# Layer 3's chunk sums in bf16: adjacency rows read in place with a stride, weights in three bf16 pieces

## The chip, the cores and the metric

The kernel runs on one core of one Trainium2 chip. The metric is the device time of one execution in microseconds (us). The kernel before takes 864.41 us as the median of three runs (862.12 to 865.53). TensorE is called PE below, VectorE DVE, ScalarE ACT, GpSimd POOL, and SyncE, which only issues transfers here, SP.

## The reference, cut to what matters

The program is a graph network of four layers over 2708 nodes with 128 features; the adjacency `adj` holds only zeros and ones. Each layer takes a normalised and rectified copy of `x` and adds its result to `x`. The change is in the last layer:

```
h     = max(layernorm(x), 0)
XW    = h @ W
s_col = XW @ a[:128];  s_row = XW @ a[128:]
den   = exp(leaky_relu(s_row[:, None] + s_col[None, :], 0.01))
num   = adj @ den
att   = where(num != 0, den / num, 0)
x     = x + adj @ (att @ XW)
```

`den` is not formed in full. Its entry for row i and column j is the exponential of s_row[i] + s_col[j] where that sum is positive, and of a hundredth of it elsewhere, so it factors on either side of a threshold. The kernel sorts the nodes by s_row into 22 chunks. For a column j, whole chunks lie on one side of the threshold and need only sums that do not depend on j; one chunk is cut by the threshold and is computed exactly. Those sums are the chunk sums: for each of the 22 chunk edges, the sum over the adjacency's rows of `exp(0.01 r)` times the rows below the edge, and of `exp(r)` times the rows above it. That is one product of a 44-column weight matrix with the transposed adjacency.

## The kernel before, in words

The nodes are held as T = 22 tiles of 128 (the last has 20). Layers 0, 1 and 2 come first; a flag then chooses between two copies of the rest, and the profiled execution takes the one with `exact` true, in which every adjacency entry is exactly representable in bf16.

Layer 3 runs in these steps. Ranks are counted (lines 728 to 776). From the ranks come the masks `ge` and `lt` (lines 791 and 793, 22 by 22 or 23 per partition) and the weights `wts` (lines 794 and 795): mask times `r_low` or `r_exp`, in f32. Then `sums(t)` (lines 798 to 816) loads one row tile of the transposed adjacency, 128 by 2708 in f32, over SP's queue, and multiplies it with `wts[:, t, :]`: six f32 matmuls of 44 weight columns and some 452 moving columns. They go to three banks of PSUM, `accs`; each bank has a lower half at partition 0 and an upper half at partition 64, and the two matmuls of a bank use different columns of the array.

The rows have four kinds of place. The first four tiles use `early_rows`, buffers that are free early. Tiles 8, 19 and 20 (`LATER`) use the buffers `hs`, `hT` and `row_b`, the last two of which are needed before for the tables. The rest take turns in the four buffers of `steps`.

Beside the sums runs a long chain, mostly of small DVE instructions: the first table (`placed("k", ...)`, line 870: products on DVE, then 22 matmuls at line 854), its reading (`joined`), the chunk edges (matmul, line 875), a count of the columns per chunk (lines 880 to 899), a plan that packs the columns into steps (lines 924 to 1005), the second table (`placed("j", ...)`, line 1008), and the indices of rows and prefix sums. Then `densities` (lines 1070 to 1091) makes 44 small matrices in 11 calls, four at a time: a product on DVE (line 1074), an f32 matmul (line 1081) into one of two PSUM banks, and its evacuation by DVE and ACT in turn (lines 1087 and 1089), a maximum and an exponential. Lines 1093 to 1100 call densities, the remaining sums and the gathers of adjacency rows. When the last sum is done, `accs` is copied out, cut in a high and a low part (lines 1107 to 1111) and sent to DRAM (`pre_d`, line 1114). The loop over 22 steps that follows (from line 1125) needs rows gathered out of `pre_d` before it can begin; it ends with the products of lines 1191 and 1135. A last product with the adjacency (line 225) finishes the layer.

The order of the instructions on each engine is set by a planner: it walks the program with its own costs, and gives an engine the earliest instruction in program order among those that it holds to be ready. Later ones can so slip in where an engine would be idle. A few stages are kept in program order by hand; the stage of the change is not.

`pieces` (line 832) cuts an f32 vector into bf16 parts: a cast, a subtraction of the cast from the rest, and so on. It is used before for the two tables.

Of the kernel before, what the change touches and what calls it, by code (L numbers as in the profile page):

```python
# [8 lines left out]
F32 = mybir.dt.float32  # L9
BF16 = mybir.dt.bfloat16  # L10
# [4 lines left out]
ALU = mybir.AluOpType  # L15
AX = mybir.AxisListType
# [3 lines left out]
def kernel(  # L20
# [19 lines left out]
    nc = tc.nc  # L40
    P = 128
    N, D = x.shape
    assert D == P
    T = -(-N // P)
# [6 lines left out]
    BLK = list(zip(CUTS[:-1], CUTS[1:]))  # L51
# [10 lines left out]
    def rows(t):  # L62
        return min(P, N - t * P)
# [23 lines left out]
    const = ctx.enter_context(tc.tile_pool(name="const", bufs=1))  # L87
    big = ctx.enter_context(tc.tile_pool(name="big", bufs=1))
    small = ctx.enter_context(tc.tile_pool(name="small", bufs=2))
    stage = ctx.enter_context(tc.tile_pool(name="stage", bufs=4))  # L90
    ps_acc = ctx.enter_context(tc.tile_pool(name="ps_acc", bufs=1, space=bass.MemoryType.PSUM))
    ps = ctx.enter_context(tc.tile_pool(name="ps", bufs=2, space=bass.MemoryType.PSUM))

# [3 lines left out]
    def acc_bank(b):  # L97
        return ps_acc.tile([P, 512], F32, tag=f"acc{b}", name=f"acc{b}")
# [59 lines left out]
    hn = big.tile([P, T, D], F32, name="hn")  # L158
    hT = big.tile([P, NPAD], F32, name="hT")
    hs = big.tile([P, T, P + 2], F32, name="hs")  # L160
    yT = big.tile([P, NPAD], F32, name="yT")
# [5 lines left out]
    dflat = big.tile([P, max(2 * N, NS * P)], F32, name="dflat")  # L167
# [107 lines left out]
    with ExitStack() as stack:  # L275
# [23 lines left out]
        for b in range(NB):  # L299
            layernorm(b, hn)  # L300
            p = bank()
            turned(p, hn, TILES[b])
            nc.vector.tensor_copy(hT[:, spans(b)], p[:, : len(TILES[b]) * P])
            p = acc_bank(b % 2)
            w = len(TILES[b]) * P
# [28 lines left out]
        accs = [acc_bank(b) for b in range(NB)]  # L334
# [13 lines left out]
        for t in range(T):  # L348
            a = first_rows[t] if t < 3 else load_rows(adj, t)
            late = t >= T - 2  # L350
            rhs = (yT, row_b)[t % 2]
            for h, (h0, h1) in enumerate(COLS):
                w = h1 - h0
# [11 lines left out]
                for b in range(3 * h, 3 * h + 3):  # L365
                    lo, hi = E0[b]
# [5 lines left out]
                        start=(t == 0 and b < GR),  # L372
                        stop=(t == T - 1 and b >= GR),
# [24 lines left out]
        p = bank()  # L398
# [36 lines left out]
    CH = P - len(SUMS)  # L435
    NC = T
# [10 lines left out]
    by_ch = iota("by_ch", [P, NC + 1], [[CH, NC + 1]], 0)  # L447
# [39 lines left out]
    def rest(exact, stack3):  # L487


        s12 = stack3.enter_context(ExitStack())  # L490
        ring = s12.enter_context(tc.tile_pool(name="ring", bufs=6))
        raws = s12.enter_context(tc.tile_pool(name="raws", bufs=4))
        h2 = hs[:, :, :P]
        if exact:
            parts = s12.enter_context(tc.tile_pool(name="parts", bufs=1))
# [73 lines left out]
        def finish1(b, acc):  # L569
            evacuate(b, yT, acc)  # L570
            n = len(TILES[b])
            p = bank()
            o = stage.tile([P, 4, P], F32, tag="o", name="o", bufs=2)
            for q, t in enumerate(TILES[b]):
                nc.tensor.matmul(p[:, cols(q)], yT[:, cols(t)], w1_sb, start=True, stop=True)
            for q, t in enumerate(TILES[b]):
                nc.scalar.activation(o[:, q, :], p[:, cols(q)], AF.Relu, scale=dis[:, t : t + 1])
            ts = slice(TILES[b][0], TILES[b][-1] + 1)
            nc.vector.tensor_add(xs[:, ts, :], xs[:, ts, :], o[:, :n, :])
            layernorm(b, h2)  # L580
            if b >= 3:
                cut_in_two(h2, b)
# [52 lines left out]
        steps = stack3.enter_context(tc.tile_pool(name="steps", bufs=4))  # L635
# [8 lines left out]
        r_exp = keepers.tile([P, T], F32, name="r_exp")  # L644
# [10 lines left out]
        regained = [b[:, :N] for b in (hT, row_b, hs.rearrange("p t w -> p (t w)"), yT)]  # L655
# [13 lines left out]
        with tc.tile_pool(name="tab", bufs=1) as tab, tc.tile_pool(name="tabs", bufs=2) as tabs:  # L669

            def tt(name, shape, a, b, op, dtype=F32, tag=None):
                o = tab.tile(shape, dtype, tag=tag or name, name=name)
                nc.vector.tensor_tensor(o, a, b, op)
                return o
# [12 lines left out]
            for b in range(NB):  # L687
                lo, hi = E0[b]
                n = len(TILES[b])
                ts = slice(TILES[b][0], TILES[b][-1] + 1)  # L690
                nc.scalar.activation(yT[:, lo:hi], row_b[:, lo:hi], AF.Relu, bias=tot[:, 6:7], scale=tot[:, 5:6])
                p = acc_bank(b % 2)
                turned(p, yT, TILES[b], True)
                f = len([t for t in TILES[b] if t < TF])
# [8 lines left out]
                p = acc_bank(2 + b % 2)  # L703
# [10 lines left out]
                for c in range(new.start, new.stop, 3):  # L714
# [8 lines left out]
                    p = acc_bank(4)  # L723
# [5 lines left out]
            for c in range(0, T, 3):  # L729
# [9 lines left out]
                for q in range(m):  # L739
                    t = c + q  # L740
                    r = rows(t)
# [14 lines left out]
                    o = (t % 4) * P  # L756
# [5 lines left out]
            p = bank()  # L762
# [4 lines left out]
            rank = tab.tile([P, T], F32, name="rank")  # L767
# [12 lines left out]
            r_low = tab.tile([P, T], F32, name="r_low")  # L780
# [1 line left out]
            nc.vector.tensor_scalar_mul(row_a[:, :N], row_b[:, :N], -0.99)  # L782


            def over(x, n):
                return x[:, :, None].to_broadcast([P, T, n])

            def along(x, n):
                return x[:, None, :].to_broadcast([P, T, n])

            ge = tt("ge", [P, T, NC + 1], over(rank, NC + 1), along(by_ch, NC + 1), ALU.is_ge)
            wts = tab.tile([P, T, 2 * NC], F32, name="wts")
            lt = tt("lt", [P, T, NC], over(rank, NC), along(by_ch[:, :NC], NC), ALU.is_lt, tag="w3")
            nc.vector.tensor_mul(wts[:, :, :NC], lt, over(r_low, NC))
            nc.vector.tensor_mul(wts[:, :, NC:], ge[:, :, 1:], over(r_exp, NC))
            accs = [acc_bank(b) for b in range(3)]

            def sums(t):
                r = rows(t)
                if t < NEARLY:  # L800
                    a = early_rows[t]
                elif t in LATER:
                    a = regained[LATER[t]]
                else:
                    a = steps.tile([P, N], F32, tag="rows", name="rows")
                nc.sync.dma_start(a[:r, :], adj_t[t * P : t * P + r, :])
                for b in range(3):
                    for h in range(2):
                        lo, hi = BLK[b + 3 * h]
                        nc.tensor.matmul(  # L810
                            accs[b][64 * h : 64 * h + 2 * NC, : hi - lo],
                            wts[:r, t, :],
                            a[:r, lo:hi],
                            start=(t == 0),
                            stop=(t == T - 1),
                        )

            early_rows = [dflat[:, :N], dflat[:, N : 2 * N], hn.rearrange("p t d -> p (t d)")[:, :N], yT[:, :N]]
            NEARLY = len(early_rows)

            LATER = {NEARLY + 4: 2, T - 3: 0, T - 2: 1}
            for t in range(NEARLY):
                sums(t)


            ohc = tt("ohc", [P, T, NC], ge[:, :, :NC], ge[:, :, 1:], ALU.subtract)
            nth = tab.tile([P, T], F32, name="nth")
            nc.vector.tensor_reduce(nth, ge[:, :, 1:NC], AX.X, ALU.add)
            slot = tab.tile([P, T], F32, name="slot")
            nc.vector.scalar_tensor_tensor(slot, nth, float(-CH), rank, ALU.mult, ALU.add)  # L830

            def pieces(name, x, n):
                out = []
                for i in range(n):
                    h = tab.tile([P, T], BF16, name=f"{name}{i}")
                    nc.vector.tensor_copy(h, x)
                    out.append(h)
                    if i < n - 1:
                        rest = tab.tile([P, T], F32, name=f"{name}r{i}")
                        nc.vector.tensor_sub(rest, x, h)  # L840
                        x = rest
                return out

            def placed(name, onehot, lanes, groups, p):

                w = len(sum(groups, [])) * NC
                hs_ = lanes[:, : T * P].rearrange("p (t q) -> p t q", q=P)
                nc.vector.tensor_tensor(hs_, along(place_of if name == "k" else lane, P), over(slot, P), ALU.is_equal)
                lo = 0 if name == "k" else 5 * NC * T
                rhs = row_b.bitcast(BF16)[:, lo : lo + T * w].rearrange("p (t s) -> p t s", s=w)  # L850
                for i, v in enumerate(sum(groups, [])):
                    nc.vector.tensor_mul(rhs[:, :, i * NC : (i + 1) * NC], onehot, over(v, NC))
                for t in range(T):
                    nc.tensor.matmul(p[:, :w], hs_[:, t, :], rhs[:, t, :], start=(t == 0), stop=(t == T - 1))

            def joined(dst, p, at, n):

                if n == 1:
                    nc.vector.tensor_copy(dst, p[:, at * NC : (at + 1) * NC])
                else:  # L860
                    nc.vector.tensor_reduce(
                        dst, p[:, at * NC : (at + n) * NC].rearrange("p (i b) -> p b i", b=NC), AX.X, ALU.add
                    )
# [5 lines left out]
            p = acc_bank(3)  # L869
            placed("k", ohc, hT.bitcast(BF16)[:, :NPAD], [r_p, node_p], p)  # L870
            ktab = tab.tile([P, 2 * NC], F32, name="ktab")
            joined(ktab[:, :NC], p, 0, 3)
            joined(ktab[:, NC:], p, 3, 2)
            p = acc_bank(4)
# [10 lines left out]
            p = acc_bank(3)  # L885
# [6 lines left out]
            for t in range(T - 1):  # L892
# [4 lines left out]
                    start=False,  # L897
# [20 lines left out]
            def sums_before(name, x):  # L918
# [66 lines left out]
                tag="w3",  # L985
# [327 lines left out]
```

## Time and profile before

| | us |
|---|---|
| median of three runs | 864.41 |
| the profiled execution | 862.16 |
| its span, first to last instruction | 860.4 |
| layer 3 from the masks to the first table's matmuls | 441.65 to 455.09 |
| from there to the first density's product | 455.09 to 494.67 |
| densities and remaining sums | 495.4 to 524.8 |
| copy-out, store, gather, first product of the loop | 524.8 to 543.6 |
| loop of 22 steps | 543.6 to 787.5 |
| last product and output | 787.5 to 860.4 |

| engine | busy us | share |
|---|---|---|
| PE | 737.2 | 86% |
| DVE | 580.9 | 68% |
| ACT | 536.0 | 62% |
| POOL | 191.8 | 22% |

The shares are over the whole span. The chunk sums (line 810) appear as 528 matmul records, two for each of 264 f32 matmuls. In the profile's answers, "idle before <- X" names what ended an engine's wait; "issue" means that it waited for nothing that the profile shows; x counts instructions. A window's row gives, for each engine, its busy us and in brackets its instructions, then the granted PE clock, the busy share of the DMA engines and the GB/s that they moved.

### The profile page before, as it was taken

What the parts mean: (1) busy time and instruction counts of PE and PEld (TensorE: products, weight loads), DVE (VectorE), ACT (ScalarE), POOL (GpSimd) and SP (SyncE); (2) the same over time, 40 slices, a digit from 0 to 9 for tenths busy, and PEclk for the clock granted to TensorE, in tenths of its full rate; (3) what the DMA queues carried; (4) which work ended last, traced back from release to release, by engine and by line L of the source; (5) the groups of instructions that cost most, each with busy time, mean ns of one, the idle gap of its engine ahead of it and who ended that gap; (6) DMA issues with size and microseconds to landing.
All of it is one profiled execution on the core that took longest, in us unless ns stands there. A gap on an engine that the chain in (4) does not pass through costs nothing.

```text
span 860.4 us, 8730 instructions
## 1 busy us (share of the span) xinstructions
PE 737.2 (86%) x2981; PEld 427.3 (50%) x2981; DVE 580.9 (68%) x1098; ACT 536.0 (62%) x595; POOL 191.8 (22%) x161
## 2 busy tenths in 40 slices
PE   3599999995996989978669893599998999989996
PEld 2333333333775867755224221456555555545785
DVE  5499879796734263458986974566666676665854
ACT  3899999995846474446940043578777777777000
POOL 3000000013201020011000101656666666620010
PEclk9899999996998989978769997799999999999999
DMA  9044544724997999967304956677777777786994
GB/s 335 3 163 161 194 172 164 291 75 172 385 397 257 361 362 396 367 260 270 115 1 178 417 203 238 235 283 261 267 271 257 274 276 270 285 313 251 421 428 132
DMA packets 39474, 218.61 MB, mean 254 GB/s; under 512 B 5107, under 2 KB 13998, under 8 KB 25358
## 3 DMA queue, kind: packets, MB, share of 16 engines
q1 hardware_dynamic: 27704, 150.19, 45.5%
q0 software_dynamic: 8624, 65.76, 21.2%
q10 hardware_dynamic: 3090, 1.99, 0.7%
q8 instruction: 26, 0.43, 0.2%
q14 instruction: 30, 0.25, 0.1%
HBM read 214.12 MB, written 3.79 MB: 253 GB/s over the span
## 4 chain that ended last, share of the span: by engine, by line
PE 17%; DMA 11%; DVE 10%; issue 6%; POOL 5%; ACT 5%; POOLq 0%; DVEq 0%; ACTq 0%
PE bank L1191 5%; DMA hs<-in_adj_t_dram 4%; PE acc L1135 4%; DMA row_b<-pre_d,pre_i 4%; PE acc L810 3%; ACT rows L1153 2%; PE acc L225 2%; PE bank L1081 2%; POOL hs L647 1%; POOL hT L647 1%; DVE bits L744 1%; POOL xw L647 1%; POOL row_b L647 1%; ACT e L1205 1%; DMA hs<-in_adj_t_dram,row_i 1%
## 5 line engine op out<-in xcount | busy, mean ns | idle before, releaser
L1191 PE MATMUL bank<-rows,d_hi 128*128 128x512 f32 (+1 forms) x264 | 105.6, 404 | 37.9 <-DVE d_hi L1160 17.4
L225 PE MATMUL acc<-rows,h_hi 128*128 128x512 f32 (+1 forms) x264 | 105.8, 405 | 11.6 <-ACT rows L529 6.3
L1135 PE MATMUL acc<-e,xw 128*128 128x512 f32 (+1 forms) x264 | 104.3, 545 | 0.0
L1196 ACT ACTIVATE ln<-bank,tiny 128x512 f32<-128x512 f32 x132 | 79.5, 632 | 31.1 <-PE bank L1191 31.1
L225 PE MATMUL acc<-rows,h_lo 128*128 128x512 f32 (+1 forms) x264 | 97.7, 386 | 0.2 <-DVE h_lo L506 0.2
L1191 PE MATMUL bank<-rows,d_lo 128*128 128x512 f32 (+1 forms) x264 | 97.4, 380 | 0.0
L1191 PEld LDWEIGHTS bank<-rows,d_hi 128*128 128x128 f32 x264 | 50.6, 192 | 67.3 <-ACT ln L1196 30.3
L1199 DVE TENSOR_TENSOR e<-e,ln 128x1536 f32<-128x1536 f32 (+2 forms) x66 | 69.7, 1096 | 14.8 <-ACT ln L1196 14.4
L359 DVE SCALAR_TENSOR_TENSOR tau<-tau,e_hi,a 128x1536 f32<-128x1536 f32 (+1 forms) x44 | 70.5, 1622 | 9.9 <-DMA a<-in_adj_dram 6.0
L1135 PEld LDWEIGHTS acc<-e,xw 128*128 128x128 f32 x264 | 48.5, 190 | 52.6 <-issue 52.6
L356 ACT ACTIVATE tau<-row_a,e_neg,e_lo 128x1536 f32<-128x1536 f32 (+1 forms) x44 | 65.7, 1504 | 3.0 <-PE bank L368 2.8
L225 PEld LDWEIGHTS acc<-rows,h_hi 128*128 128x128 f32 x264 | 52.1, 198 | 26.0 <-ACT rows L529 8.6
L368 PE MATMUL bank<-tau,ones_at 128*32 128x512 f32 (+1 forms) x264 | 51.8, 566 | 8.3 <-DVE tau L359 8.3
L225 PEld LDWEIGHTS acc<-rows,h_lo 128*128 128x128 f32 x264 | 52.0, 198 | 11.7 <-issue 1.9
L1205 ACT ACTIVATE e<-e 128x2708 f32<-128x2708 f32 x22 | 54.2, 2462 | 3.2 <-DVE e L1199 3.2
L225 PE MATMUL acc<-yT,hs 128*128 128x512 f32 x132 | 55.8, 560 | 0.0
L225 PE MATMUL acc<-row_b,hs 128*128 128x512 f32 x132 | 55.3, 557 | 0.0
L1191 PEld LDWEIGHTS bank<-rows,d_lo 128*128 128x128 f32 x264 | 51.0, 193 | 6.7
L225 PE MATMUL acc<-rows,y_hi 128*128 128x512 f32 x132 | 49.2, 379 | 4.6 <-DVE rows L1268 2.7
L225 PE MATMUL acc<-rows,y_lo 128*128 128x512 f32 x132 | 47.7, 376 | 0.0
L1174 DVE TENSOR_SCALAR xw<-xw,c_exp 128x128 f32<-128x128 f32 x22 | 6.3, 285 | 60.4 <-DMA xw<-xw_d,xw_i 60.4
L529 ACT CAST rows<-dflat 128x1536 fp32r<-128x1536 f32 (+1 forms) x26 | 34.2, 1330 | 20.2 <-DMA dflat<-in_adj_t_dram 9.7
(409 smaller groups left out, 1414.7 us busy)
## 6 DMA issues: line engine op xcount, KB each, us to landing
a<-in_adj_dram SPq DMA_DIRECT2D x21, 1354.0 KB
rows<-in_adj_t_dram SPq DMA_DIRECT2D x17, 1354.0 KB
dflat<-in_adj_t_dram SPq DMA_DIRECT2D x9, 768.0 KB
rows<-in_adj_t_dram SPq DMA_DIRECT2D x9, 768.0 KB
dflat<-in_adj_dram SPq DMA_DIRECT2D x9, 768.0 KB
rows<-in_adj_dram SPq DMA_DIRECT2D x9, 768.0 KB
dflat<-in_adj_t_dram SPq DMA_DIRECT2D x5, 1354.0 KB
hs<-in_adj_t_dram SPq DMA_DIRECT2D x5, 1354.0 KB
```

The costliest lines, as they stand in the source:

```text
L225: nc.tensor.matmul(accs[b][:, : hi - lo], w, moving[:, lo - at : hi - at], start=start and i == 0, stop=stop and i == len(parts) - 1,)
L356: nc.scalar.activation(tau[:, :w], row_a[:, h0:h1], AF.Relu, bias=e_neg[:, t : t + 1], scale=e_lo[:, t : t + 1])
L359: nc.vector.scalar_tensor_tensor(tau[:, :w], tau[:, :w], e_hi[:, t : t + 1], a[:, h0:h1], ALU.add, ALU.mult)
L368: nc.tensor.matmul(den[g : g + 32, : hi - lo], ones_at[:, b // GR, :], tau[:, lo - h0 : hi - h0], start=(t == 0 and b < GR), stop=(t == T ...
L529: m = nc.vector.tensor_copy(r, a) if i % 2 and i > 4 else nc.scalar.copy(r, a)
L647: return nc.gpsimd.indirect_dma_start(out=out, out_offset=None, in_=src, in_offset=bass.IndirectOffsetOnAxis(ap=idx, axis=0),)
L810: nc.tensor.matmul(accs[b][64 * h : 64 * h + 2 * NC, : hi - lo], wts[:r, t, :], a[:r, lo:hi], start=(t == 0), stop=(t == T - 1),)
L1135: m = nc.tensor.matmul(accs[b][:, : hi - lo], xw, e[:, lo:hi], start=(s == 0), stop=(s == NE - 1))
L1191: m = nc.tensor.matmul(num[:, : hi - lo], d, a[:, lo:hi], start=(i == 0), stop=(i == len(products) - 1))
L1196: nc.scalar.activation(ln[:, lo:hi], num[:, : hi - lo], AF.Ln, bias=tiny)
L1199: tc.keep_in_program_order(nc.vector.tensor_sub(e[:, beg:hi], e[:, beg:hi], ln[:, beg:hi]))
L1205: tc.keep_in_program_order(nc.scalar.activation(e, e, AF.Exp))
```

## The change

In the exact branch the chunk sums no longer use f32 operands. The upper 16 bits of an f32 zero or one are that number in bf16, so the loaded tile is read in place as bf16, every second element: a stride of two elements, four bytes. The weights `r_low` and `r_exp` are cut by `pieces` into three bf16 parts each, and three weight tensors `wts0` to `wts2` are built, each 44 columns wide. A bank of a row tile then takes six bf16 matmuls (three parts, two halves) where it took two in f32.

`pieces` is moved up so that it can be called there. The loop that calls `sums` for the first four tiles, with their loads, moves down: in program order it now stands behind the first table's products and matmuls, between the allocation of `ktab` and the reading of the table. The pool `stage`, which held the tile `o` of layer 1's finish, is replaced by a pool `relus` of the same two buffers, opened with the pools of layers 1 and 2.

```diff
-    stage = ctx.enter_context(tc.tile_pool(name="stage", bufs=4))
...
+        relus = s12.enter_context(tc.tile_pool(name="relus", bufs=2))
...
-            o = stage.tile([P, 4, P], F32, tag="o", name="o", bufs=2)
+            o = relus.tile([P, 4, P], F32, tag="o", name="o")
...
             ge = tt("ge", [P, T, NC + 1], over(rank, NC + 1), along(by_ch, NC + 1), ALU.is_ge)
-            wts = tab.tile([P, T, 2 * NC], F32, name="wts")
             lt = tt("lt", [P, T, NC], over(rank, NC), along(by_ch[:, :NC], NC), ALU.is_lt, tag="w3")
-            nc.vector.tensor_mul(wts[:, :, :NC], lt, over(r_low, NC))
-            nc.vector.tensor_mul(wts[:, :, NC:], ge[:, :, 1:], over(r_exp, NC))
+            values = [(r_low, r_exp)]
+            if exact:
+                values = list(zip(pieces("r_low_p", r_low, 3), pieces("r_exp_p", r_exp, 3)))
+            wts = []
+            for i, (v_low, v_exp) in enumerate(values):
+                w = tab.tile([P, T, 2 * NC], BF16 if exact else F32, name=f"wts{i}")
+                nc.vector.tensor_mul(w[:, :, :NC], lt, over(v_low, NC))
+                nc.vector.tensor_mul(w[:, :, NC:], ge[:, :, 1:], over(v_exp, NC))
+                wts.append(w)
...
                 nc.sync.dma_start(a[:r, :], adj_t[t * P : t * P + r, :])
+                if exact:
+                    a = a.bitcast(BF16).rearrange("p (n h) -> p n h", h=2)[:, :, 1]
                 for b in range(3):
-                    for h in range(2):
-                        lo, hi = BLK[b + 3 * h]
-                        nc.tensor.matmul(
-                            accs[b][64 * h : 64 * h + 2 * NC, : hi - lo],
-                            wts[:r, t, :],
-                            a[:r, lo:hi],
-                            start=(t == 0),
-                            stop=(t == T - 1),
-                        )
+                    for i, w in enumerate(wts):
+                        for h in range(2):
+                            lo, hi = BLK[b + 3 * h]
+                            nc.tensor.matmul(
+                                accs[b][64 * h : 64 * h + 2 * NC, : hi - lo],
+                                w[:r, t, :],
+                                a[:r, lo:hi],
+                                start=(t == 0 and i == 0),
+                                stop=(t == T - 1 and i == len(wts) - 1),
+                            )
...
-            for t in range(NEARLY):
-                sums(t)
...
             placed("k", ohc, hT.bitcast(BF16)[:, :NPAD], [r_p, node_p], p)
             ktab = tab.tile([P, 2 * NC], F32, name="ktab")
+            for t in range(NEARLY):
+                sums(t)
             joined(ktab[:, :NC], p, 0, 3)
```

More of the change, by code (lines that the diff above doesn't have):

```diff
@@ L782, in rest @@
             nc.vector.tensor_scalar_mul(row_a[:, :N], row_b[:, :N], -0.99)
[L785 to L791, printed above, removed]
-            wts = tab.tile([P, T, 2 * NC], F32, name="wts")
-            lt = tt("lt", [P, T, NC], over(rank, NC), along(by_ch[:, :NC], NC), ALU.is_lt, tag="w3")
-            nc.vector.tensor_mul(wts[:, :, :NC], lt, over(r_low, NC))
-            nc.vector.tensor_mul(wts[:, :, NC:], ge[:, :, 1:], over(r_exp, NC))
[L796 to L807, printed above, removed]
-                    for h in range(2):
-                        lo, hi = BLK[b + 3 * h]
-                        nc.tensor.matmul(
-                            accs[b][64 * h : 64 * h + 2 * NC, : hi - lo],
-                            wts[:r, t, :],
-                            a[:r, lo:hi],
-                            start=(t == 0),
-                            stop=(t == T - 1),
-                        )
-            early_rows = [dflat[:, :N], dflat[:, N : 2 * N], hn.rearrange("p t d -> p (t d)")[:, :N], yT[:, :N]]
-            NEARLY = len(early_rows)
-            LATER = {NEARLY + 4: 2, T - 3: 0, T - 2: 1}
-            for t in range(NEARLY):
-                sums(t)
[L826 to L830, printed above, removed]
             def pieces(name, x, n):
@@ L842, in pieces, with over, along @@
                 return out
+            def over(x, n):
+                return x[:, :, None].to_broadcast([P, T, n])
+            def along(x, n):
+                return x[:, None, :].to_broadcast([P, T, n])
+            ge = tt("ge", [P, T, NC + 1], over(rank, NC + 1), along(by_ch, NC + 1), ALU.is_ge)
+            lt = tt("lt", [P, T, NC], over(rank, NC), along(by_ch[:, :NC], NC), ALU.is_lt, tag="w3")
+            values = [(r_low, r_exp)]
+            if exact:
+                values = list(zip(pieces("r_low_p", r_low, 3), pieces("r_exp_p", r_exp, 3)))
@@ new lines, in rest, with sums @@
+            wts = []
[4 more added lines that the diff above has]
+                wts.append(w)
+            accs = [acc_bank(b) for b in range(3)]
+            def sums(t):
+                r = rows(t)
+                if t < NEARLY:
+                    a = early_rows[t]
+                elif t in LATER:
+                    a = regained[LATER[t]]
+                else:
+                    a = steps.tile([P, N], F32, tag="rows", name="rows")
+                nc.sync.dma_start(a[:r, :], adj_t[t * P : t * P + r, :])
+                if exact:
+                    a = a.bitcast(BF16).rearrange("p (n h) -> p n h", h=2)[:, :, 1]
+                for b in range(3):
+                    for i, w in enumerate(wts):
[8 more added lines that the diff above has]
+                            )
@@ new lines, in rest @@
+            early_rows = [dflat[:, :N], dflat[:, N : 2 * N], hn.rearrange("p t d -> p (t d)")[:, :N], yT[:, :N]]
+            NEARLY = len(early_rows)
+            LATER = {NEARLY + 4: 2, T - 3: 0, T - 2: 1}
+            ohc = tt("ohc", [P, T, NC], ge[:, :, :NC], ge[:, :, 1:], ALU.subtract)
+            nth = tab.tile([P, T], F32, name="nth")
+            nc.vector.tensor_reduce(nth, ge[:, :, 1:NC], AX.X, ALU.add)
+            slot = tab.tile([P, T], F32, name="slot")
+            nc.vector.scalar_tensor_tensor(slot, nth, float(-CH), rank, ALU.mult, ALU.add)
```

## The prediction

> **What bounds the kernel now.** I read the stages first. One row each for the early sums, the middle and the density stage; columns are PE, PEld, DVE, ACT, POOL busy, PE clock, DMA share, GB/s:
>
> ```profile
> 444.05:455.10 11.05, 10.99 (x49) 3.40 (x49) 7.07 (x10) 0.00 (x0) 0.00 (x0) 0.84 0.01 1
> 457.20:495.40 38.20, 33.85 (x211) 13.07 (x210) 36.37 (x101) 0.22 (x1) 4.06 (x4) 1.00 0.86 343
> 495.40:524.80 29.40, 29.33 (x94) 8.15 (x94) 21.36 (x43) 15.85 (x34) 3.00 (x3) 0.94 0.52 192
> ```
>
> Three different limits. In the first PE is full (10.99 of 11.05). In the second DVE is (36.37 of 38.20) and DMA nearly so; PE's 33.85 lies beside them. In the third PE is full again (29.33 of 29.40). Then the chain of waits (start, duration):
>
> ```profile
> 444.11 11.06 PE acc L810 x48
> 455.16 1.21 PE acc L854 x22
> 456.37 0.89 PE acc L810 x2
> ...
> 494.67 0.70 DVE diag L1074
> 495.42 3.68 PE bank L1081 x4
> 499.10 1.64 PE acc L810 x6
> 500.74 1.05 PE bank L1081 x2
> ```
>
> The sums of line 810 are on the path twice: four early tiles ahead of the first table, and the last six tiles (72 records) amid the densities. Last, PE and DVE in order of time:
>
> ```profile
> 448.55 0.12 PEld L810 LDWEIGHTS acc<-dflat,wts 128*44 128x44 f32 x2 [0.26 <-issue]
> ...
> 449.31 0.13 PEld L810 LDWEIGHTS acc<-dflat,wts 128*44 128x44 f32 x2 [0.25 <-issue]
> 449.68 0.13 PEld L810 LDWEIGHTS acc<-dflat,wts 128*44 128x44 f32 x2 [0.25 <-issue]
> ...
> 449.89 1.23 DVE L852 TENSOR_TENSOR row_b<-ohc,node_p 128x484 bf16<-128x484 f32 x2
> ...
> 522.27 2.48 PE L810 MATMUL acc<-rows,wts 20*44 20x452 f32 x12
> ```
>
> Two weight loads, one per half bank, start together every 0.377 us (448.55, 449.31, 449.68). So the halves run side by side, and a tile (12 records, six rounds) costs 6 x 0.377 = 2.26 us. The early tiles cost more since the first rounds ran at the low clock, 0.75 us each until 447.8. The first table's DVE products end at 451.12, but its matmuls start at 455.09: they stood 4.0 us behind the early sums.
>
> **The Trainium skill.** "FP8 and Floating Point Precision", TensorE Precision Notes: true f32 takes four passes, bf16 one. The trace agrees: two records of 0.377 are four passes of 0.188 us for 452 columns. "TensorE: Matmul & The Clock Gate", "Wait — 56ns, not 53.3ns?": one pass costs N / 2.4 GHz + 2.5 ns warm, so 0.191 us; the 0.188 agrees. "Advanced Engine Details and Errata", SBUF Cachelines: a stride is free while there are at least two hits on a 16-byte line. A stride of four bytes has four hits, so I expect full pace; no bf16 read with a stride is in this trace. "TensorEngine Tiling (Array Packing)", Key Properties: different tiles can load weights and multiply in parallel. The f32 pairs do.
>
> **The change part by part.**
>
> Pool `relus`: same two buffers, used only in layer 1; nothing.
>
> Pieces: six casts and four subtractions. The rows of r_p (line 836) last 0.18 us and start some 0.1 apart, so 1.0 us, from when r_exp and r_low exist (409.6, 410.5 us). There ACT's row sums (line 747) run without a break to 439.7 and DVE waits for them. Nothing; 1.0 to 1.8 us if that cover is gone.
>
> Weights: six products for two. The f32 pair starts 0.57 apart (442.82, 443.39); bf16 products of that size (line 852) last the same 0.66. Four more are +2.3 us on DVE ahead of the first table, which becomes ready at 451.1 + 2.3 = 453.4. The 4.0 us that it waited for PE hide this only if PE is free by then.
>
> Early sums: 4 tiles x 9 rounds x 0.19. The first weights exist at about 444.0, the third at 446.3. With the low clock to 447.8 about 6 of 36 rounds are done by then, and 30 x 0.19 = 5.7 us bring the end to 453.5. The text puts the table's matmuls first, but they are not ready. The planner fills an idle PE: at 456.3 it set sums of a late tile ahead of line 875's matmul, which precedes them in the program. So I expect most early sums before the table. Its matmuls then start at 453.5 against 455.09: -1.6 us. Whatever sums the planner leaves between the table and the chunk-edge matmul (line 875) hold that one up, and behind it the whole DVE chain to 494.67. All 72 there: PE idle, low clock for the table (+1.2) and the first sums (+0.9), 6.8 us of sums: 453.4 + 1.3 + 8.9 = 463.6 against 457.19, +6. Bounds -1.6 to +6; I take -1.6. Their loads (four issues on SP) move down in the text too, but they went out at 364 to 402 us as buffers came free, ahead of all rows but the first `steps` ones; nothing.
>
> Middle, 457 to 495: DVE's chain and the transfers set it (DMA 0.98 or more from 469 on). Faster sums free the four `steps` buffers 2 to 3 us earlier, so rows land earlier; nothing on the chain.
>
> Density stage: PE's 29.3 us are 13.0 of line 1081 (3.68 cold for two, then about 1.05 each for nine) and 16.4 of sums. A tile now costs 9 x 0.19 = 1.71. I expect one tile of the six to have gone ahead, with rows landing earlier: 5 x 1.71 = 8.55, plus 1.0 for the changes between kinds (three matmuls took 1.65, not 1.51, at each of some eight places) = 9.6. Stage: 13.0 + 9.6 = 22.6, so -6.7. If none goes ahead: 10.3 + 1.0 + 13.0 = 24.3, -5.0. The next limit is the evacuation of the two banks by DVE and ACT: two densities back to back took 518.05 to 521.6, 1.8 each, so 3.7 + 9 x 1.8 + the last tile 1.7 = 21.6, -7.7. It is just below.
>
> After it, copy-out, store and gather (18.8 us), loop (243.9) and last product start earlier by the same amount: they hang on the last sum, not on a clock or a transfer of their own.
>
> Sum: -1.6 - 6.7 = -8.3. Span 860.4 becomes 852.1, with the 1.8 around it 853.9 against 862.2. That execution is 2.25 below the median of the runs, so against 864.4 I predict 856.1.
>
> **The rivals.**
>
> *More of the gain*: the late sums no longer wait for PE at all; what remains is their transfers. DMA was full to about 505, and the last rows would land at about 502, so the last sum could end at 505 to 511 instead of 524.3, -13 to -18: 849. For it: early freed buffers. Against: the planner set the last three tiles behind densities 8, 10 and 11, by when it held their rows to be there.
>
> *The table does not gain*: the early sums stand between the first table and line 875, +6. The densities then start at 500.7 and finish bound by evacuation, 500.7 + 21.6 = 522.3 against 524.3: -2, 862. For it: the program order. Against: the planner's filling.
>
> *Slower: the bf16 passes do not run at 0.19 per round*. One cause decides: the strided read at half pace, 0.377 per round. A tile costs 3.39. Early sums: 30 rounds at 0.377 end at 459 and hold line 875 by +2 to +3. In the middle 12 tiles need 40.7 us where 35 are there, so about two more tiles (6.8) fall into the density stage, whose own six cost 6 x 1.13 = 6.8 more. Part hides behind evacuation: about +12, 876. It decides from 2.26 / 9 = 0.25 us per round. Against: the cited rule, and f32 passes that stream four bytes per column at 0.188. Halves that do not overlap give the same.
>
> *The planner's order*: it has 18 instructions per tile to place for six. If its price for one is over a third of an f32 one, it sends fewer tiles ahead of the densities; two or three more left (3.4 to 5.1 us) and evacuation-bound densities give -3 to +4: 865.
>
> That the change does nothing would need the sums off the path; the full PE row of the third stage speaks against.
>
> **How the numbers follow.** Likeliest case 0.46, its own range 850 to 860; more gain 0.12; no gain at the table 0.18; half pace 0.12; order 0.08; the rest 0.04. The likeliest gives 856.1. From 846 (864.4 - 18) to 868 (+4) all but the half-pace case, a little of the order and of the rest lies inside. About 0.5%, 4.3 us, is what a measurement tells from no change. Faster: nine tenths of 0.46, all of 0.12, a sixth of 0.18: 0.57. Slower: 0.12, two thirds of 0.08, bits of the rest: 0.21. Same: 0.22.
>
> **What would show it.** Line 810's weight loads 0.19 us apart in pairs at full clock (0.377 or single file: slower rival). Line 854's first matmul at about 453.5 and line 875's within 2.5 us of it (over 5: sums between). The first `diag` at about 493. Fewer than six tiles of sums after it, and the last sum 21 to 24 us later. The wait before line 1191 shifted, not grown. I am wrong if the rounds are slow, if sums stand before line 875, or if the loop's start does not follow the last sum.

## The result

| | before | changed |
|---|---|---|
| median of 20 runs each, us | 864.21 (860.80 to 869.32) | 860.94 (857.63 to 864.66) |
| profiled execution's span, us | 860.4 | 859.1 |
| chunk-sum matmul records on PE | 264 | 396 |

The ratio is 0.9968 (95% interval 0.9953 to 0.9984): 2.8 us faster by the ratio, 3.3 by the medians. I had forecast 8.3. The kernel before has 264 matmul records for its sums, two for each of 132 f32 matmuls; the 528 given above counted the 264 weight loads with them.

The masks of layer 3 (`ge`) start at 441.65 us before and at 443.45 after. In the eleven profiled executions of this study they start between 441.31 and 444.07, with no relation to the edits, so I count layer 3 from there:

| us after the masks' start | before | changed | difference | forecast |
|---|---|---|---|---|
| first table's matmuls | 13.44 | 11.90 | -1.54 | -1.6 |
| chunk-edge matmul | 15.54 | 13.61 | -1.93 | |
| first density's product on DVE | 53.02 | 50.39 | -2.63 | -1.6 |
| end of the last sum | 83.10 | 78.85 | -4.25 | -8.3 |
| store of the prefix sums begins | 88.16 | 84.14 | -4.02 | |
| first product of the loop | 100.50 | 97.86 | -2.64 | -8.3 |
| end | 418.75 | 415.65 | -3.10 | -8.3 |

The stage of densities and remaining sums in the changed kernel, as a window (PE, PEld, DVE, ACT, POOL busy, PE clock, DMA share, GB/s):

```profile
494.59:522.30 27.71, 27.29 (x148) 10.09 (x148) 21.45 (x43) 15.60 (x34) 2.08 (x2) 0.94 0.57 225
```

PE is as full as before (27.29 of 27.71) and the stage is only 1.6 us shorter than the 29.3 of before. The chain of waits of the changed kernel (start, duration; line 833 is the sums, 862 the table, 1091 the densities):

```profile
447.05 8.36 PE acc L833 x61
455.41 1.21 PE acc L862 x22
...
493.84 0.70 DVE diag L1084
494.59 3.68 PE bank L1091 x4
498.27 1.30 PE acc L833 x11
499.57 1.06 PE bank L1091 x2
...
509.88 2.13 PE acc L833 x18
512.01 1.92 PE bank L1091 x4
513.92 1.93 PE acc L833 x18
515.85 1.07 PE bank L1091 x2
```

The table now starts 0.1 us after the last of its DVE products (455.35 against 455.22). But the densities alternate with blocks of 11 sums at 1.30 us where before they alternated with blocks of three f32 sums at 1.65. From 494.59 on there are 126 bf16 matmuls, seven row tiles; before there were 72 records, six tiles. And a whole tile of 18 takes 1.93 us there, not 1.71. PE's timeline shows that it stood idle just before:

```profile
485.03 5.53 PE L833 MATMUL acc<-rows,wts 128*44 128x450 bf16 x39
494.59 3.68 PE L1091 MATMUL bank<-diag,ones 128*128 128x512 f32 x4 [4.03 <-DVE diag L1084]
```

For 4.03 us PE waited for the first density, with the next tile of sums placed behind it.

After the last sum, one thing takes time back. The store of the prefix sums, from the chain of the kernel before and then of the changed one:

```profile
529.81 6.39 DMA pre_d<-yT
```

```profile
527.59 7.80 DMA pre_d<-yT
```

It starts 4.0 us sooner, counted from the masks, but lasts 1.4 us longer, and the loop begins only 2.64 us sooner.

### The profile page after: what moved, and what is told of

Same layout as the page of the kernel before. It is cut to its first block, busy times and chain, and to the rows that moved or that the text cites. A ratio compares the mean times of both kernels' runs of the same rounds, so it can differ in the third digit from the quotient of the medians.

```text
span 859.1 us, 9007 instructions
## 1 busy us (share of the span) xinstructions
PE 727.6 (85%) x3113; PEld 436.7 (51%) x3113; DVE 583.0 (68%) x1112; ACT 535.8 (62%) x595; POOL 193.5 (23%) x161
## 4 chain that ended last, share of the span: by engine, by line
PE 12%; DMA 10%; DVE 10%; POOL 7%; issue 7%; ACT 6%; POOLq 0%; DVEq 0%; ACTq 0%
DMA hs<-in_adj_t_dram 4%; DMA yT<-pre_d,pre_i 4%; PE acc L1145 3%; PE bank L1201 3%; PE acc L833 2%; ACT rows L1163 2%; POOL hT L647 2%; PE acc L224 2%; POOL hs L647 2%; POOL yT L647 1%; PE bank L1091 1%; POOL xw L647 1%; ACT row_a L747 1%; ACT e L1215 1%; DVE bits L744 1%
## 5 line engine op out<-in xcount | busy, mean ns | idle before, releaser
L358 DVE SCALAR_TENSOR_TENSOR tau<-tau,e_hi,a 128x1536 f32<-128x1536 f32 (+1 forms) x44 | 70.5, 1623 | 10.2 <-DMA a<-in_adj_dram 5.5
L529 ACT CAST rows<-dflat 128x1536 fp32r<-128x1536 f32 (+1 forms) x26 | 34.2, 1330 | 20.7 <-DMA dflat<-in_adj_dram 11.6
L173 POOL TENSOR_TENSOR rstd<-isq,neg_half 128x4 f32<-128x4 f32 (+1 forms) x24 | 23.5, 982 | 99.8 <-DVE isq L172 85.0
```

The lines of the kernel that those rows point to most:

```text
L173: nc.gpsimd.tensor_tensor(dst, s[:, :n], neg_half[:, :n], ALU.pow)
L358: nc.vector.scalar_tensor_tensor(tau[:, :w], tau[:, :w], e_hi[:, t : t + 1], a[:, h0:h1], ALU.add, ALU.mult)
L529: m = nc.vector.tensor_copy(r, a) if i % 2 and i > 4 else nc.scalar.copy(r, a)
```

## The experiments

**Which half of the edit gains.** One kernel keeps the bf16 sums and puts the early loop back ahead of the table:

```diff
             LATER = {NEARLY + 4: 2, T - 3: 0, T - 2: 1}
+            for t in range(NEARLY):
+                sums(t)
...
             ktab = tab.tile([P, 2 * NC], F32, name="ktab")
-            for t in range(NEARLY):
-                sums(t)
```

> The changed kernel with the four early sums put back ahead of the first table; the bf16 sums stay. Theory A: moving the early sums let the table start 1.5 us sooner, but put one tile of sums more behind the first density (the instruction order of this kernel has 16 tiles ahead of it, that of the changed kernel 15). So here the first table starts within 0.5 us of the changed kernel's, counted from the masks, because PE is done with the early sums when DVE is done with the table's products; six tiles instead of seven are left, the last sum ends 1.5 to 2 us sooner, and the kernel is 1 to 2 us faster than the changed one, ratio to before 0.994 to 0.996. Theory B: the move is what gained at the table; without it the table waits for PE as before, and the kernel is 1 to 2 us slower than the changed one, ratio 0.998 to 0.999.

Measured: 858.15 us against 864.26, ratio 0.9942 (0.9924 to 0.9959). Theory A held. From PE's timeline of this kernel:

```profile
493.28 3.61 PE L1091 MATMUL bank<-diag,ones 128*128 128x512 f32 x4 [2.63 <-DVE diag L1084]
496.81 1.19 PE L833 MATMUL acc<-rows,wts 128*44 128x452 bf16 x9
497.93 1.12 PE L1091 MATMUL bank<-diag,ones 128*128 128x512 f32 x2
498.98 1.18 PE L833 MATMUL acc<-rows,wts 128*44 128x452 bf16 x9
...
516.73 2.00 PE L833 MATMUL acc<-rows,wts 20*44 20x452 bf16 x18
```

Blocks of nine, not eleven; six tiles are left, and the stage takes 25.45 us instead of 27.7. The table starts 12.43 us after the masks (11.90 in the changed kernel, 13.44 before), and the last sum ends at 77.14, 1.7 us sooner than with the move. Its interval and the changed kernel's overlap only from 0.9953 to 0.9959; the medians, each against its own runs of before, are 6.1 and 3.3 us faster.

The other kernel keeps f32 and makes only the move.

> The kernel before, f32 sums, with only the early loop moved behind the first table. Theory A: the table starts 4 us sooner, but 11 of the 24 f32 matmuls now stand between it and the chunk-edge matmul (5.5 pairs of 0.754 us, 4.1 us), so the edge matmul comes only some 0.7 us sooner; 15 tiles instead of 16 lie ahead of the first density, and the one more costs 2.3 us there: 1 to 2 us slower than before, ratio 1.001 to 1.003. Theory B: the move alone brings what the table gained: 1.5 to 2 us faster than before, ratio about 0.998.

Measured: 866.10 us, ratio 1.0029 (1.0011 to 1.0047): slower, as theory A said. Its PE timeline around the table:

```profile
452.72 1.28 PE L852 MATMUL acc<-row_b,hT 128*128 128x110 bf16 x22
453.92 1.72 PE L810 MATMUL acc<-hn,wts 128*44 128x452 f32 x8
...
456.23 2.44 PE L810 MATMUL acc<-yT,wts 128*44 128x452 f32 x10
458.60 0.40 PE L875 MATMUL acc<-ktab,first 128*128 128x22 f32 x2
```

The table starts 9.62 us after the masks, 3.8 sooner, but the sums behind it hold the edge matmul until 15.50, where it was before (15.54). The move gains nothing there with f32 sums. Seven tiles are left amid the densities, as in the changed kernel, and the last sum ends at 84.38 against 83.10. So the move puts one tile behind the densities whatever the type of the sums, and the bf16 sums carry the whole gain.

**Why a tile took 1.93 us and not 1.71.** The strided read, replaced by a contiguous one of the same size (it reads other halves of the data, so its sums are not the right ones):

```diff
                 if exact:
-                    a = a.bitcast(BF16).rearrange("p (n h) -> p n h", h=2)[:, :, 1]
+                    a = a.bitcast(BF16)[:, :N]
```

> The changed kernel with the sums reading the first 2708 bf16 halves of a tile without a stride, instead of every second one: same sizes and counts, other data, so its output is not the reference's. If the stride of four bytes is why a round of two bf16 matmuls took 0.200 us and not 0.188, rounds take 0.188 to 0.191 here and the kernel is 0.5 to 1.5 us faster than the changed one. If it is the loading of weights or the issue of four instructions per round, rounds stay at 0.200 and the time at that of the changed kernel.

Measured: ratio 0.9947 (0.9926 to 0.9969), 859.58 us. The interval overlaps that of the changed kernel, so the time says little; the traces are clear. An early tile in a row of others, first in the changed kernel, then with the contiguous read:

```profile
451.80 0.36 PE L833 MATMUL acc<-hn,wts 128*44 128x452 bf16 x1
...
453.60 0.36 PE L833 MATMUL acc<-yT,wts 128*44 128x452 bf16 x1
```

```profile
449.99 0.35 PE L833 MATMUL acc<-hn,wts 128*44 128x452 bf16 x1
...
451.71 0.35 PE L833 MATMUL acc<-yT,wts 128*44 128x452 bf16 x1
```

From one tile's first matmul to the next one's: 1.80 us strided, 1.72 contiguous, so nine rounds of 0.200 and 0.191. The stride costs about 5%. The other 0.13 of the 1.93 is the change between sums and densities: with the contiguous read, too, a whole tile amid the densities takes 1.84 us, 0.12 more than in a row of others.

**Where the 1.4 us at the store went.** `hs` is free long before `hT` and `row_b`, but is gathered last. This kernel gathers it first:

```diff
-            for q in range(3):
+            for q in (2, 0, 1):
                 gather_rows(regained[q], q)
```

> The changed kernel, with the first three gathers of adjacency rows in the order hs, hT, row_b instead of hT, row_b, hs: the buffer hs is free long before the others. Theory A: the prefix sums' store took 7.8 us instead of 6.4 because the rows' gathers of row_b and hs were still on the DMA engines. With hs gathered some 25 us earlier the store lasts about 5 us, and the loop starts 2 to 3 us sooner than in the changed kernel: ratio to before 0.993 to 0.995. Rival: the store's length is its own (short pieces), and the time equals that of the changed kernel, ratio 0.996 to 0.998.

Measured: 860.28 us, ratio 0.9957 (0.9936 to 0.9977). In its profile the store shortened as theory A said, and the loop starts 2.4 us sooner (95.44 us after the masks, 97.86 in the changed kernel):

```profile
526.22 5.65 DMA pre_d<-yT
```

So rows still being gathered lengthen the store. In the time it does not show: the interval holds the changed kernel's ratio. Of the 2.4 us the profile keeps 1.4 at the end (414.2 after the masks against 415.65).

**Whether the end hangs on the last sum.** If it does, densities set behind it should pay. The order of the late tiles and densities is written by hand, and PE is held to it by `tc.keep_in_program_order` on the sums from tile 15 on and on all densities (not shown in the diff): tiles 4 to 16, two densities, then 17, 18, 19 with one density after each, 20 and 21, and the other six densities.

```diff
-            for s0 in range(0, FIRST, 4):
-                densities(s0)
-            for t in range(NEARLY, T):
-                sums(t)
+            late_steps = [*range(NEARLY, T - 5), "d", "d", T - 5, "d", T - 4, "d", T - 3, "d", T - 2, T - 1]
+            s0 = 0
+            for step_of in late_steps:
+                if step_of == "d":
+                    densities(s0)
+                    s0 += 4
+                else:
+                    sums(step_of)
...
-            for s0 in range(FIRST, NS, 4):
+            for s0 in range(s0, NS, 4):
                 densities(s0)
```

> The changed kernel with PE's order of the late sums and densities written by hand: tiles 4 to 16 ahead of all densities, then two densities, tile 17, one density, tile 18, one density, tile 19, one density, tiles 20 and 21, and six densities after the last sum. Theory A: the end hangs on the last sum; the planner put all 11 densities (13.0 us of PE) ahead of it. Here five densities (6.9 us) and five tiles lie between the first density and the end of the sums: about 6.9 + 5 x 1.9 = 16 us instead of 27.7, rows landing by about 506, so the last sum ends 10 to 12 us sooner. The six densities fit into the 18 us of copy-out, store and gather. The kernel is 8 to 11 us faster than the changed one, ratio to before 0.983 to 0.988. Rival: the remaining densities (DVE 2.0 us each, 12 us) or the loop's own gathers hold the loop's start, and less than 4 us remain, ratio 0.992 or more.

Measured: 855.06 us against 864.58, ratio 0.9884 (0.9860 to 0.9907), some 7 us faster than the changed kernel; just under what theory A gave. The last sum ended 68.61 us after the masks, 10.2 sooner, as expected. PE's timeline:

```profile
485.72 7.31 PE L835 MATMUL acc<-rows,wts 128*44 128x450 bf16 x57
494.17 2.00 PE L835 MATMUL acc<-rows,wts 128*44 128x452 bf16 x18 [1.14 <-DMA rows<-in_adj_t_dram]
```

The 57 matmuls are the 39 of the changed kernel and tile 15 behind them, without a wait. Tile 15 begins at 490.9, 13.1 us after its load went out (477.78). In the changed kernel that load went out at 478.09; by the same interval its rows would have been there at 491.2, with 3.4 us of PE's idle 4.03 left. The first two densities also take 1.98 us here (496.10) instead of 3.68: after the idle 4.03 us the granted PE clock in them was 0.53, here it is 1.00.

The first product of the loop came only 5.3 sooner (92.56). Two of the five lost are in the store, which took 7.80 us in the changed kernel:

```profile
517.60 9.81 DMA pre_d<-yT
```

The other three lie between the store's end and the loop's first product: 9.2 us (527.41 to 536.63) against 5.9 in the changed kernel (535.39 to 541.31). In this stretch the later densities now run on DVE and ACT. The stretch takes 5.7 to 6.0 us in the six kernels that have no density behind the sums, and 9.0 to 11.6 in the four with six densities there whose store stands on the chain. That ties it to the order; which of the densities' instructions holds the loop up was not shown.

The same order with the f32 sums of the kernel before:

> The kernel before, f32 sums in their old place, with the same order of late tiles and densities written by hand. Theory A: order is what counts, and bf16 adds only its share: five densities 6.9 us and five tiles of 2.4 us end the sums 19 us after the first density instead of 29.3, so 8 to 10 us faster than before, ratio 0.988 to 0.991. Rival: with f32 sums PE cannot take 13 tiles ahead of the first density, which starts later, and the gain is under 4 us, ratio over 0.995.

Measured: 858.11 us, ratio 0.9925 (0.9902 to 0.9948), between the two accounts. The last sum ends at 71.31, 11.8 sooner than before, but the loop starts 5.0 sooner: here too over half is lost on the way. Order alone gains more than the change under study did. The kernel above is 3 us faster (855.06 against 858.11), but it has the move as well.

And with bf16, the order, and the early loop in its old place:

> bf16 sums, the early loop ahead of the table as in the kernel before, and the order written by hand. Theory A: with the order fixed, the tile that the move cost is no longer left to the planner, so this equals the changed kernel with hand order within 1 us, ratio 0.983 to 0.988. Rival: the move costs something beside that tile, and this is 2 us or more faster than the changed kernel with hand order.

Measured: 852.72 us, ratio 0.9874 (0.9849 to 0.9900), against 855.06 with the move. Whether the 2.3 us are real stays open, since the intervals overlap. This kernel and the f32 one with the same order differ in the change under study without its move: 852.72 against 858.11, 5.4 us for bf16, with intervals that do not overlap. PE's timeline of this kernel:

```profile
505.79 1.99 PE L835 MATMUL acc<-row_b,wts 128*44 128x452 bf16 x18 [0.56 <-DMA row_b<-in_adj_t_dram]
507.72 1.99 PE L835 MATMUL acc<-rows,wts 20*44 20x452 bf16 x18
509.63 1.98 PE L1095 MATMUL bank<-diag,ones 128*128 128x512 f32 x4
515.86 4.26 PE L1095 MATMUL bank<-diag,ones 128*128 128x512 f32 x4 [4.25 <-DVE diag L1088]
```

The sums now wait for rows once (0.56 us), and end at 66.70. The other densities run while the sums are copied out and stored. The loop starts at 88.31, against 100.50 before.

Two last kernels combine this with another order of gathers, `hs` first and then `hs` second.

> The same with the first three gathers of adjacency rows in the order hs, hT, row_b. Theory A: the store of the prefix sums lasts 2 us less, as it did with the planner's order (5.65 against 7.80), and the loop starts 2 us sooner: ratio 0.981 to 0.986. Rival: the first steps of the loop are held by their own gathers, and what the store gains is given back there: the same time as without it.

Measured: 852.27 us, ratio 0.9852 (0.9826 to 0.9877), the same as without it within the intervals. Theory A's gain is not there in the time, and not for the rival's reason either:

```profile
501.85 2.00 PE L835 MATMUL acc<-rows,wts 128*44 128x452 bf16 x18 [2.70 <-DMA rows<-in_adj_t_dram]
503.78 1.13 PE L1095 MATMUL bank<-diag,ones 128*128 128x512 f32 x2
505.72 2.01 PE L835 MATMUL acc<-hT,wts 128*44 128x452 bf16 x18 [0.81 <-DMA hT<-in_adj_t_dram]
```

The gather of `hs`, now at 490.79, takes its turn on DMA engines that were full with row tiles. Tile 18 arrives late and the last sum ends 3.8 us later, at 70.47. The store does seem shorter: the first gather from it goes out 6.94 us after its last issue, against 8.38 without this edit.

> bf16 sums, early loop ahead of the table, order written by hand, and the first gathers in the order hT, hs, row_b. With hs first, its gather fell among the last rows' loads and delayed the last sum by 3.8 us. Here it follows hT's, when the rows have landed. Theory A: the last sum ends where it does without the gather's move (66.7 us after the masks), only row_b's gather is still ahead of the store, the store lasts 5 to 6 us instead of 7.46, and the loop starts 1.5 to 2 us sooner than in that kernel: ratio 0.982 to 0.987. Rival: by then the loop's start hangs on the densities and casts on DVE, and the time is that without the gather's move, ratio 0.987 or more.

Measured: 852.83 us, ratio 0.9864 (0.9819 to 0.9908), which both accounts allow. The trace bears out neither. The last sum ends at 68.31, 1.6 us later than without the edit (66.70), where theory A had it unchanged, and the loop starts at 90.31, 2.0 later (88.31).

```profile
514.35 7.54 DMA pre_d<-yT
522.79 3.46 DMA hT<-pre_d,pre_i
526.27 1.67 DVE rows L1172
527.94 0.65 DVE dflat L1105
```

The store is as long as without the edit (7.54 against 7.46), so theory A's gain is missing, and densities stand on the chain once (527.94). Kernels at 852 to 853 us, some 8 us below the changed one, are the fastest of this study; which of the three is fastest, the runs do not tell.

## Why the prediction was right or wrong

**The early sums and the table: right.** Forecast -1.6, measured -1.54, by the mechanism given: the planner filled PE with 69 of the 72 early matmuls before the table, so the rival with sums between table and edge matmul did not come about for bf16. It came about for f32 (9.62 for the table, 15.50 for the edge matmul). The four added weight products did come ahead of the table, at 0.57 us each. But this gain is not the move's: in the four bf16 kernels without the move the table starts at 11.8 to 12.4, in the four with it at 11.8 to 11.9.

**The DVE chain: a little better than forecast.** The edge matmul came 1.93 us sooner, and from there to the first density another 0.7 us went, so the gain there was 2.63, not 1.6. Why stays open.

**The density stage: this step failed.** "I expect one tile of the six to have gone ahead" gave five tiles and 22.6 us. The stage took 27.7. Seven tiles were left, two more than assumed: at 14.3 us of PE for seven tiles (2.04 each with the changes between kinds; forecast 9.6 for five, 1.92 each) the two are 3.8 us, the dearer tiles 0.9 and an idle of 0.4 the rest. The kernel without the move, with six left, took 25.45, where the forecast for six was 24.3. The forecast followed the transfers, and these did allow it: tile 15's load went out 3.0 us sooner than before (34.6 us after the masks against 37.6), and by the hand-ordered kernel's figures its rows would have been there while PE stood idle ahead of the first density. But PE executes in the order that the planner wrote, and the planner set fewer tiles ahead of the densities, 15 and not 16. The outcome is close to the fourth rival's, "two or three more left" (one more than before, two more than assumed), but not from its cause: the f32 kernel with the move left seven tiles as well, and the bf16 kernel without it six. The move cost the tile, not the number or the price of the bf16 instructions, and the prediction had put the move at nothing in this stage. Why the planner lost one with it was not found.

**The price of a round: 5% off.** I took 0.19 because the Trainium skill, "Advanced Engine Details and Errata", SBUF Cachelines, asks for two hits on a 16-byte line for full pace, and a stride of four bytes has four. Measured 0.200 strided and 0.191 contiguous. The measurement decides: nearly free, and far from the half pace of the slower rival. That bf16 needs a single pass is shown by the same 0.191.

**After the last sum: this step failed too.** "They hang on the last sum, not on a clock or a transfer of their own." The store hangs on the gathers of rows ahead of it as well: the last sum came 4.25 us sooner, the loop 2.64, and 1.4 of the difference is the longer store. With the hand order 10.2 became 5.3, of which the store took 2.0 and the stretch with the later densities 3.3.

**What held of the whole:** that the last sum is on the path. Moving densities behind it paid 7 us on top of the change, and would have been the larger gain. The measured 860.9 lies just above the likeliest case's 850 to 860; the wider range from 846 to 868 held it, but not for the reason that the forecast gave.

## What to carry to other kernels

When a full engine takes its work in an order that a planner wrote, a cheaper instruction gains only what the new order leaves of it: count the work that stands ahead of the gate in the new order, rather than in the old one. Ask first whether all of the work ahead of the gate belongs there; here six densities did not, and moving them gained more than the cheaper passes. And follow the gain through the next transfer: here a store behind queued gathers kept 1.4 us of 4.25.

## What the runs showed of the hardware that I had not expected

A bf16 moving operand read with a stride of four bytes cost 0.200 us per round of two matmuls of some 452 columns, against 0.191 contiguous.

The store of the prefix sums, four transfers of 233 KB, lasted from 5.65 to 9.81 us with the same bytes: 5.65 where one of the three gathers of rows had been done long before, and 6.39 to 9.81 with all three shortly ahead of it. In the six of the latter whose traces show when the last gather (`hs`) landed, that was 4.2 to 7.9 us after the store's start, and the store, 7.37 to 9.81 us long, ended 1.9 to 3.6 us after it. The two go together; that this is why the lengths differ was not shown by an edit.

After 4.03 us without work, PE was granted a clock of 0.53 in the first two densities of the changed kernel, and they took 3.68 us; straight behind a tile of sums, in the hand-ordered kernel, it was 1.00 and they took 1.98.
